# Masked attention after a group normalization: group statistics by transposes and GpSimd sums, and a split of the score products in two visits

## The chip, the cores and the metric

One core of one Trainium2 chip runs the whole kernel. Its engines are TensorE (PE in the profile, with PEld for its weight loads), VectorE (DVE), ScalarE (ACT), GpSimd (POOL) and SyncE (SP). Each takes its instructions in program order from its own queue, and they wait for each other by semaphores. The metric is the device time of one execution in microseconds (us), as the median of several runs.

## What is computed

The input is x, 32 images of 256 channels and 32 x 32 pixels in float32. A group normalization over 32 groups of 8 channels comes first, then attention of 8 heads of 32 channels with a strictly lower mask, and the input is added to the result:

```python
def _gn(v, G=32, eps=1e-5):                      # 8 channels x 1024 pixels a group
    g = v.reshape(B_, G, C_ // G, H_, W_)
    m = jnp.mean(g, axis=(2, 3, 4), keepdims=True)
    s = jnp.var(g, axis=(2, 3, 4), keepdims=True)
    return ((g - m) / jnp.sqrt(s + eps)).reshape(v.shape)

q, k, v = ...                                     # 1x1 convolutions with bias
scores = jnp.einsum('bhqd,bhkd->bhqk', q, k) / jnp.sqrt(dk)
attn = softmax(where(mask == 0, -10000, scores)); attn = where(mask == 0, 0, attn)
out = jnp.einsum('bhqk,bhkd->bhqd', attn, v)
return x + out
```

A channel is a partition, and the 256 channels are two tiles of 128 (g = 0, 1). So a group is 8 neighbouring partitions, and its statistics need a sum over partitions. Mean and variance of each channel come first. The group's mean is the mean of the channels' means, and its variance is the mean of the channels' variances plus the mean of the squared deviations of their means.

## The kernel before

An image is worked off in 12 visits: 6 for each half of the heads (4 heads, g = 0, 1). The main loop (L750 to L769) runs over all 384 visits and one more. At step i it emits the scores of visit i, then what is planned `at` i (a projection of the next image, above all), then the values of visit i - 1, then what is planned `between`, then the additions of keys of visit i - 1, and at last what is planned `after` i. The order is written out by hand for all five engines (`tc.manual_schedule`), so what stands earlier in this program stands earlier in each engine's queue.

**A visit.** `scores` (L348) computes transposed scores of 4 heads into three PSUM tiles: heads 0, 1 long, heads 2, 3 long, and the short remainders of all four. A product of one head takes 32 rows of PE and 64 of its columns, in two halves, so several run side by side. The order is: short products of heads 2, 3; long ones of heads 0, 1; long ones of heads 2, 3; a wait until the first short ones are done (`bank_free`, L379); short products of heads 0, 1. Where a visit has two long entries and is in `PAIRS` (visits 0 and 6), one long entry of heads 0, 1 stands between the two short ones of heads 2, 3 (L364). ACT takes three exponentials of each visit (L397 twice, L393). In visits 0, 1, 3, 4 of each half, `mask` (L329) has POOL make a triangle of the diagonal blocks by two selects (L339), one for each 128 columns. `values` (L412) multiplies the exponentials with v on PE; the diagonal products come after the others, each behind its select. `add_keys` (L434) sums exponentials on DVE (L440), and POOL's DMAs fold these sums over partitions (`fold`, L449). `finish` (L539) normalizes with the inverse sums and adds x, on DVE.

**Preparation of the next image.** `prepare` (L637) plans it over the visits of the image before, by `PREPARE` (L652): channel statistics of g = 0 and 1 on DVE after visits 0 and 1 (`norm_channels`, L179); the product with `avg` that gives the groups' means between values and additions of step 3 (`norm_mean`, L187: PE, then ACT writes minus the mean); the deviations on DVE in the same place (`norm_deviation`, L198); a second product and ACT's copy after step 4 (`norm_variance`, L210); the power -1/2 and the shift on POOL, also after step 4 (`norm_rstd`, L221); and from step 5 ACT's normalization of x (`norm_apply`, L231), whose results the projections take from step 7. The product with `avg` is four PE instructions of 128 rows by 32 columns; each is done in two passes, so the profile counts eight.

The selects of a visit are emitted with its scores. What POOL is given `after` step 2 or 3 therefore stands in its queue ahead of the selects of visit 3 or 4, and behind those of the visits up to then. At step 3, `after` also holds the second fold of an earlier image's last sum, which is planned first.

The tile `turned` (L465, one buffer) holds transposed sums in steps 6 and 7.

Of the kernel before, what the change touches and what calls it, by code (L numbers as in the profile page):

```python
# [32 lines left out]
def tile_norm_attention_residual(  # L33
# [65 lines left out]
    def unshifted():  # L99
# [79 lines left out]
        def norm_channels(b, g):  # L179
            if g == 0:  # L180
                live["mv", b] = small.tile([P, NG, 2], F32, tag="mv", name=f"mv_{b}")
            st = small.tile([P, NH, 6], F32, tag="st", name=f"st_{b}_{g}")
            for c in range(NH):
                nc.vector.bn_stats(st[:, c, :], live["x", b][:, g, c * HALF : (c + 1) * HALF])
            nc.vector.bn_aggr(live["mv", b][:, g, :], st)

        def norm_mean(b):  # L187
            mv = live["mv", b]
            pm = misc(f"pm_{b}")
            product(pm[:, :NG], avg, mv[:, :, 0])  # L190
            if b == 0:
                live["dev", b] = small.tile([P, NG], F32, tag="dev", name=f"dev_{b}")
                nc.vector.tensor_sub(live["dev", b], mv[:, :, 0], pm[:, :NG])
            mean = small.tile([P, NG], F32, tag="mean", name=f"mean_{b}")
            nc.scalar.activation(mean, pm[:, :NG], AF.Identity, scale=-1.0)
            live["minus_mean", b] = mean

        def norm_deviation(b):  # L198
            mv, minus_mean = live["mv", b], live["minus_mean", b]

            if b == 0:
                dev = live["dev", b]
            else:
                dev = small.tile([P, NG], F32, tag="dev", name=f"dev_{b}")
                nc.vector.tensor_add(dev, mv[:, :, 0], minus_mean)
            nc.vector.tensor_mul(dev, dev, dev)
            nc.vector.tensor_add(dev, dev, mv[:, :, 1])
            live["dev", b] = dev

        def norm_variance(b):  # L210
# [4 lines left out]
            if b == 0:  # L215

                nc.vector.tensor_scalar_add(rstd, pv[:, :NG], 1e-5)
                return
            nc.scalar.activation(rstd, pv[:, :NG], AF.Identity, bias=eps)

        def norm_rstd(b):  # L221
            rstd = live["rstd", b]
            if b == 0:

                nc.gpsimd.tensor_tensor(rstd, rstd, power, ALU.pow)
                return
            nc.gpsimd.tensor_tensor(rstd, rstd, power, ALU.pow)
# [100 lines left out]

        def mask(b, g, raw, j):  # L329
# [18 lines left out]
        def scores(b, v):  # L348
# [15 lines left out]
            if i in PAIRS and len(longs) > 1:  # L364
# [227 lines left out]
        PAIRS = {0: 0, 1: 1, 3: 3, 4: 2}  # L592

# [38 lines left out]
        at, between, after = {}, {}, {}  # L632
# [4 lines left out]
        def prepare(b, whens):  # L637
            for n, f in zip(whens, [
                lambda: norm_channels(b, 0), lambda: norm_channels(b, 1), lambda: norm_mean(b),
                lambda: norm_deviation(b), lambda: norm_variance(b), lambda: norm_rstd(b),  # L640
            ] + [lambda hf=hf, g=g: norm_apply(b, hf, g) for hf in range(NH) for g in range(NG)]):
                if n is None:
                    f()
                elif isinstance(n, tuple):
                    when(n[0], f, between)
                else:
                    when(n, f, after)
# [4 lines left out]
        PREPARE = (-12, -11, -9, -9, -8, -8, -7, -6, -5, -3)  # L652
# [4 lines left out]
        every = range(4)  # L657
        ALIGN = 24, 64

        with tc.manual_schedule(engines={ENG.PE, ENG.Activation, ENG.DVE, ENG.Pool, ENG.SP}):  # L660
# [43 lines left out]
            if B > 1:  # L704
                prepare(1, (None, None, 0, 1, 2, 2, 3, 4, 5, 7))
            for b in range(B):
# [4 lines left out]
                if b >= 2:  # L711
# [6 lines left out]
                    prepare(b, [(first + n,) if k in (2, 3) else first + n for k, n in enumerate(PREPARE)])  # L718
# [31 lines left out]
            for i in range(B * N + 1):  # L750
# [8 lines left out]
                if i:  # L759
                    values(b, v)  # L760
                    for f in between.pop(i, ()):
                        f()
# [7 lines left out]
            assert not at and not between and not after  # L770
# [174 lines left out]
```

## Time and profile before

| | |
|---|---|
| Time, median of 3 runs | 1794.0 us (1793.49 to 1794.12) |
| The profiled execution | 1793.44 us, its span 1791.7 us |
| Mean granted clock of PE | 0.999 |
| One image | 55.09 us |

How to read the profile: its times are from one execution. A row of the timeline gives start, duration, engine, line, operation, the tiles written and read, how many instructions are merged, and in brackets the idle time before with what ended it. The durations of DVE and POOL include time in which an instruction had begun and could not go on. Ends of matmuls are modelled. The groups that belong to the statistics, from the list of groups by form:

```profile
L169 PE MATMUL pm<-mv,avg 128*32 128x2 f32 x256 | 7.0, 170 | 0.0
L169 PE MATMUL pv<-dev,avg 128*32 128x2 f32 x256 | 7.1, 170 | 0.5 <-ACT k L258 0.4
L195 ACT ACTIVATE mean<-pm 128x2 f32<-128x2 f32 x32 | 5.5, 172 | 29.6 <-PE pm L169 25.9 <-DVE dev L193 3.6
L219 ACT ACTIVATE rstd<-pv,eps 128x2 f32<-128x2 f32 x31 | 8.1, 263 | 13.4 <-PE pv L169 13.4
L504 DVE STREAM_TRANSPOSE inv_turned<-inv 128x64 f32<-128x64 f32 x31 | 7.6, 245 | 1.1
```

The last is a transpose that is there already; it is shown for its duration.

### The profile page before, as it was taken

The page shows a single profiled execution, that of the slowest core. Times are in us where ns is not written, and L with a number is a line of the kernel's source. Part 1 is how long each engine was busy: PE and PEld are TensorE (multiplying, and loading weights), DVE is VectorE, ACT ScalarE, POOL GpSimd, SP SyncE. Part 2 cuts the span into 40 slices and gives each one's busy share as a digit, 9 for nine tenths or more (in the row PEclk, how much of TensorE's full clock was granted, in tenths as well). Part 3 has the DMA queues.
Part 4 walks back from the last instruction along what each step waited for, and adds up shares of the span by engine and source line. Part 5 has one row for each costly group of instructions (what it writes and reads, how often), then busy time and mean ns, then how long its engine had stood idle before and what let it go on. Part 6 is the DMA issues. An engine that isn't in the chain of part 4 may idle for free.

```text
span 1791.7 us, 81825 instructions
## 1 busy us (share of the span) xinstructions
PE 1784.4 (100%) x37036; PEld 948.2 (53%) x37036; DVE 1673.4 (93%) x1826; ACT 1456.4 (81%) x1990; POOL 881.3 (49%) x903
## 2 busy tenths in 40 slices
PE   9999999999999999999999999999999999999998
PEld 5555555555555555555555555555555555555554
DVE  4689999999999999999999999999999999999998
ACT  6888878888788888788887888878888878888785
POOL 2345544554545555445554455454555544555452
PEclk9999999999999999999999999999999999999999
DMA  2566766767667766766676676767776667666664
GB/s 70 105 115 137 134 134 129 147 135 143 127 126 149 140 138 134 135 139 138 139 135 131 129 150 132 145 125 128 149 141 135 136 134 138 139 139 137 132 107 106
DMA packets 86818, 236.77 MB, mean 132 GB/s; under 512 B 21312, under 2 KB 22336, under 8 KB 70592
## 3 DMA queue, kind: packets, MB, share of 16 engines
q0 software_dynamic: 15872, 97.53, 40.1%
q1 hardware_dynamic: 70448, 133.89, 25.5%
q8 instruction: 290, 4.75, 1.1%
q14 instruction: 64, 0.52, 0.1%
q10 hardware_dynamic: 144, 0.07, 0.0%
HBM read 66.85 MB, written 34.57 MB: 57 GB/s over the span
## 4 chain that ended last, share of the span: by engine, by line
PE 99%; ACT 0%; DVE 0%; issue 0%; POOL 0%; POOLq 0%
PE sT L311 31%; PE acc L422 28%; PE pp L169 26%; PE ppv L169 13%; PE pd L474 1%; PE busy L155 0%; ACT e L397 0%; PE pv L169 0%; PE pm L169 0%; PE wt L148 0%; DVE rb_last L547 0%; ACT eh L393 0%; DVE rb_last L534 0%; DVE turned L531 0%; DVE acc L544 0%
## 5 line engine op out<-in xcount | busy, mean ns | idle before, releaser
L339 POOL TENSOR_SCALAR_AFFINE_SELECT diagonal<-eh 128x512 f32<-128x512 f32 x512 | 632.5, 1256 | 841.5 <-ACT eh L393 840.9
L397 ACT ACTIVATE e<-sT 128x1024 f32<-128x1024 f32 x768 | 744.4, 1022 | 250.3 <-PE sT L311 225.9
L440 DVE TENSOR_TENSOR e<-e,e 128x1024 f32<-128x1024 f32 x314 | 574.2, 1829 | 24.5 <-ACT v L275 3.2
L311 PE MATMUL sT<-q,k 32*64 32x128 f32 (+2 forms) x18432 | 578.4, 372 | 0.1
L311 PEld LDWEIGHTS sT<-q,k 32*64 32x64 f32 x18432 | 394.8, 131 | 188.4 <-PE sT L311 69.6
L169 PE MATMUL pp<-xn,wT 128*32 128x512 f32 x4096 | 492.2, 598 | 0.0
L422 PE MATMUL acc<-e,v 128*32 128x512 f32 (+3 forms) x4608 | 401.0, 450 | 0.0
L393 ACT ACTIVATE eh<-sT 128x768 f32<-128x768 f32 (+1 forms) x384 | 341.7, 890 | 0.0
L422 PEld LDWEIGHTS acc<-e,v 128*32 128x32 f32 x4608 | 149.2, 110 | 261.5 <-issue 238.9
L169 PE MATMUL ppv<-wT,xn 128*32 128x256 f32 x4096 | 247.5, 382 | 0.0
L440 DVE TENSOR_TENSOR diagonal<-diagonal,e 128x1536 f32<-128x1536 f32 x126 | 195.0, 1548 | 16.8 <-PE acc L422 9.2
L169 PEld LDWEIGHTS pp<-xn,wT 128*32 128x32 f32 x4096 | 107.0, 109 | 195.7 <-issue 163.7
L440 DVE TENSOR_TENSOR e<-e,eh 128x1024 f32<-128x1024 f32 x126 | 164.2, 1303 | 6.5
L422 PEld LDWEIGHTS acc<-diagonal,v 128*32 128x32 f32 x4096 | 121.1, 110 | 87.6 <-issue 76.0
L440 DVE TENSOR_TENSOR e<-e,diagonal 128x2048 f32<-128x2048 f32 x63 | 144.2, 2289 | 19.8 <-POOL diagonal L339 19.8
L169 PEld LDWEIGHTS ppv<-wT,xn 128*32 128x32 f32 x4096 | 120.1, 109 | 79.7 <-issue 7.0
L422 PE MATMUL acc<-diagonal,v 128*32 128x128 f32 x4096 | 158.7, 273 | 0.0
L244 ACT ACTIVATE xn<-x,shift,rstd 128x256 f32<-128x256 f32 x248 | 136.8, 608 | 0.6 <-POOL shift L229 0.6
L544 DVE TENSOR_TENSOR num<-num,rb 128x512 f32<-128x512 f32 x124 | 123.3, 994 | 0.2 <-DMA rb<-inverses 0.2
L453 POOL DMA_DIRECT2D e<-e x124 | 103.3, 833 | 38.2 <-issue 38.2
L547 DVE SCALAR_TENSOR_TENSOR rb<-num,v_bias_col,x 128x256 f32<-128x256 f32 x248 | 117.5, 515 | 4.4
L453 POOL DMA_DIRECT2D diagonal<-diagonal x124 | 104.1, 839 | 4.8 <-issue 4.8
(84 smaller groups left out, 984.4 us busy)
## 6 DMA issues: line engine op xcount, KB each, us to landing
x<-in_x_dram SPq DMA_DIRECT2D x124, 256.0 KB, 3.7
diagonal<-diagonal POOLq DMA_DIRECT2D x62, 512.0 KB, 5.4
e<-e POOLq DMA_DIRECT2D x62, 512.0 KB, 5.9
rb<-inverses SPq DMA_DIRECT2D x124, 256.0 KB, 3.9
out_dram<-rb SPq DMA_DIRECT2D x124, 256.0 KB, 4.9
diagonal<-diagonal POOLq DMA_DIRECT2D x62, 256.0 KB, 4.6
folded<-diagonal SPq DMA_DIRECT2D x62, 256.0 KB, 5.1
e<-e POOLq DMA_DIRECT2D x62, 256.0 KB, 5.0
```

The costliest lines, as they stand in the source:

```text
L169: nc.tensor.matmul(out[part], lhsT=lhsT[:, part], rhs=rhs, start=start, stop=stop, skip_group_check=True)
L244: nc.scalar.activation(to, of, AF.Identity, bias=live["shift", b][:, g : g + 1], scale=rstd)
L311: return nc.tensor.matmul(bank[c : c + KEYS, cols], lhsT=live["k", b, g][rows, kb * P + c : kb * P + c + KEYS], rhs=live["q", b, g][rows, ...
L339: nc.gpsimd.affine_select(out=square[:, :, place + s * P : place + (s + 1) * P], in_=raw[:, :, (1 - s) * KEYS : (3 - s) * KEYS], pattern=[ ...
L393: exp = nc.scalar.activation(eh.rearrange("p (n bank) q -> p bank n q", n=2)[:, :, :, :narrow], short[:, :, :, :narrow], AF.Exp)
L397: nc.scalar.activation(e[:, 2 * a : 2 * a + 2, :wide], pairs[a][:, :, :wide], AF.Exp)
L422: nc.tensor.matmul(acc[HD * j : HD * (j + 1), of], lhsT=live["v", b][:, kb, h * HD : (h + 1) * HD], rhs=e[:, j, :], start=first, stop=last ...
L440: nc.vector.tensor_add(to, to, tile_of(b, g, at))
L453: nc.gpsimd.dma_start(out=total[:rows], in_=total[rows : 2 * rows], accum_op=ALU.add)
L474: nc.tensor.matmul(pd[HD * j : HD * (j + 1), of], lhsT=pick, rhs=e[:, j, :], start=start, stop=stop, skip_group_check=True,)
L544: nc.vector.tensor_mul(num, num, rb)
L547: nc.vector.scalar_tensor_tensor(blocks(rb, s), blocks(num, s, (start + s) % 2 == 1), v_bias_col[:, g : g + 1], blocks(xt[:, g, cols], s), ...
```

## The change

For the images after the first (their statistics are prepared 31 times), the group sums leave PE and ACT. The channels' means and variances are written into the first 4 columns of a tile `stats` (the buffer of `turned`), whose columns up to 32 POOL has set to 0. A DVE transpose of 32 columns turns each block of 32 channels, so that the 8 channels of a group lie beside each other. `group_means` (POOL, after step 2) sums them by three additions, spreads minus the mean, subtracts and squares: six operations. `group_deviations` (POOL, after step 3) does three additions and one spreading operation. `group_variance` (DVE, also after step 3) transposes 64 columns back and subtracts. `norm_rstd` stays as it was. The first image is prepared as before.

In visits 3 and 4 of each image but the last (`SPLIT`), the long product of heads 0, 1 of 512 columns becomes one of 128 and one of 384, and the first stands between the two short ones of heads 2, 3, as in visit 0. In values of visits 2 and 8 PE gets one more wait each (`EVEN`), for a value of `bank_free` for which the scores ahead of them have waited.

```diff
         def norm_channels(b, g):
             if g == 0:
-                live["mv", b] = small.tile([P, NG, 2], F32, tag="mv", name=f"mv_{b}")
+                if b == 0:
+                    live["mv", b] = small.tile([P, NG, 2], F32, tag="mv", bufs=1, name=f"mv_{b}")
+                else:
+                    stats = live["stats", b] = small.tile([P, HALF], F32, tag="turned", bufs=1, name=f"stats_{b}")
+                    nc.gpsimd.memset(stats[:, 2 * NG : HD], 0.0)
+                    live["mv", b] = stats[:, : 2 * NG].rearrange("p (g s) -> p g s", s=2)
...
+            if b and g == NG - 1:
+                stats = live["stats", b]
+                nc.vector.transpose(stats[:, HD : 2 * HD], stats[:, :HD])
+
+        def sum_eight(b, out, of, work):
+            of = of.rearrange("p (n c) -> p n c", c=CPG)
+            half = work[:, : HD // 2].rearrange("p (n c) -> p n c", c=CPG // 2)
+            pairs = work[:, HD // 2 : 3 * HD // 4].rearrange("p (n c) -> p n c", c=CPG // 4)
+            nc.gpsimd.tensor_tensor(half, of[:, :, : CPG // 2], of[:, :, CPG // 2 :], ALU.add)
+            nc.gpsimd.tensor_tensor(pairs, half[:, :, : CPG // 4], half[:, :, CPG // 4 :], ALU.add)
+            nc.gpsimd.tensor_tensor(out, pairs[:, :, 0], pairs[:, :, 1], ALU.add)
...
+        def group_means(b):
+            of, means, dev, work = (live["stats", b][:, n * HD : (n + 1) * HD] for n in (1, 2, 6, 7))
+            sums = work[:, 3 * HD // 4 : 3 * HD // 4 + HD // CPG]
+            sum_eight(b, sums, of, work)
+            nc.gpsimd.tensor_scalar(
+                means.rearrange("p (n c) -> p n c", c=CPG), spread_of(sums), -1.0 / CPG, None, ALU.mult
+            )
+            nc.gpsimd.tensor_tensor(dev, of, means, ALU.add)
+            nc.gpsimd.tensor_tensor(dev, dev, dev, ALU.mult)
+
+        def group_deviations(b):
+            squares, dev, work = (live["stats", b][:, n * HD : (n + 1) * HD] for n in (3, 6, 7))
+            sums = work[:, 3 * HD // 4 : 3 * HD // 4 + HD // CPG]
+            sum_eight(b, sums, dev, work)
+            nc.gpsimd.tensor_scalar(
+                squares.rearrange("p (n c) -> p n c", c=CPG), spread_of(sums), 1.0 / CPG, 1e-5, ALU.mult, ALU.add
+            )
+
+        def group_variance(b):
+            stats = live["stats", b]
+            nc.vector.transpose(stats[:, 4 * HD : 6 * HD], stats[:, 2 * HD : 4 * HD])
+            means, squares = (
+                stats[:, n * HD : n * HD + 2 * NG].rearrange("p (g s) -> p g s", s=2) for n in (4, 5)
+            )
+            live["minus_mean", b] = means[:, :, 0]
+            live["rstd", b] = small.tile([P, NG], F32, tag="rstd", name=f"rstd_{b}")
+            nc.vector.tensor_sub(live["rstd", b], squares[:, :, 0], means[:, :, 1])
...
+        def part_of(b, g, bank, entry, of):
+            at, _, halves = entry
+            for j in (0, 1):
+                for ((c, kb, first, _, cols),) in halves:
+                    score(b, g, bank[:, j, :], j, (
+                        c, kb, first + of.start, of.stop - of.start, slice(cols.start + of.start, cols.start + of.stop)
+                    ))
...
             begin = [lambda n=n: long_of((0, 1), n) for n in range(len(longs) - 1, -1, -1)]
-            if i in PAIRS and len(longs) > 1:
+            if b < B - 1 and v in SPLIT:
+                begin = [lambda n=n: part_of(b, g, pairs[0], longs[0], n) for n in (slice(0, P), slice(P, HALF))]
+            if i in PAIRS and len(begin) > 1:
                 first = short_of((2, 3), begin.pop(0), slice(None, None, -1))
...
+        SPLIT = 3, 4
...
-                lambda: norm_channels(b, 0), lambda: norm_channels(b, 1), lambda: norm_mean(b),
-                lambda: norm_deviation(b), lambda: norm_variance(b), lambda: norm_rstd(b),
+                lambda: norm_channels(b, 0), lambda: norm_channels(b, 1), lambda: group_means(b),
+                lambda: group_deviations(b), lambda: group_variance(b), lambda: norm_rstd(b),
...
-        PREPARE = (-12, -11, -9, -9, -8, -8, -7, -6, -5, -3)
+        PREPARE = (-12, -11, -10, -9, -9, -8, -7, -6, -5, -3)
...
+        EVEN = 2, 8
...
-                prepare(1, (None, None, 0, 1, 2, 2, 3, 4, 5, 7))
+                prepare(1, (None, None, 0, 1, 1, 2, 3, 4, 5, 7))
...
-                    prepare(b, [(first + n,) if k in (2, 3) else first + n for k, n in enumerate(PREPARE)])
+                    prepare(b, [first + n for n in PREPARE])
...
                 if i:
+                    for _ in range(EVEN.count((i - 1) % N) if i < B * N - N else 0):
+                        nc.tensor.wait_ge(bank_free, live["free"])
                     values(b, v)
-                    for f in between.pop(i, ()):
-                        f()
```

`spread_of(sums)` is a view that repeats each sum for the 8 channels of its group.

More of the change, by code (lines that the diff above doesn't have):

```diff
@@ L185, in norm_channels, with spread_of @@
             nc.vector.bn_aggr(live["mv", b][:, g, :], st)
+            if b and g == NG - 1:
[8 more added lines that the diff above has]
+            nc.gpsimd.tensor_tensor(out, pairs[:, :, 0], pairs[:, :, 1], ALU.add)
+        def spread_of(sums):
+            return sums.unsqueeze(2).broadcast_to([P, HD // CPG, CPG])
+        def group_means(b):
[23 more added lines that the diff above has]
+            nc.vector.tensor_sub(live["rstd", b], squares[:, :, 0], means[:, :, 1])
         def norm_mean(b):
@@ L190, in norm_mean @@
             product(pm[:, :NG], avg, mv[:, :, 0])
[L191 to L194, printed above, removed]
+            live["dev", b] = small.tile([P, NG], F32, tag="dev", bufs=1, name=f"dev_{b}")
+            nc.vector.tensor_sub(live["dev", b], mv[:, :, 0], pm[:, :NG])
+            mean = small.tile([P, NG], F32, tag="mean", bufs=1, name=f"mean_{b}")
             nc.scalar.activation(mean, pm[:, :NG], AF.Identity, scale=-1.0)
@@ L198, in norm_deviation @@
         def norm_deviation(b):
[L199 to L205, printed above, removed]
+            mv, dev = live["mv", b], live["dev", b]
             nc.vector.tensor_mul(dev, dev, dev)
             nc.vector.tensor_add(dev, dev, mv[:, :, 1])
-            live["dev", b] = dev
         def norm_variance(b):
@@ L214, in norm_variance @@
             live["rstd", b] = rstd
[L215 to L219, printed above, removed]
+            nc.vector.tensor_scalar_add(rstd, pv[:, :NG], 1e-5)
         def norm_rstd(b):
             rstd = live["rstd", b]
+            nc.gpsimd.tensor_tensor(rstd, rstd, power, ALU.pow)
             if b == 0:
-                nc.gpsimd.tensor_tensor(rstd, rstd, power, ALU.pow)
                 return
-            nc.gpsimd.tensor_tensor(rstd, rstd, power, ALU.pow)
             live["shift", b] = small.tile([P, NG], F32, tag="shift", name=f"shift_{b}")
@@ L631, in unshifted @@
         }
-        at, between, after = {}, {}, {}
+        at, after = {}, {}
         def when(i, f, where=at):
@@ L643, in prepare @@
                     f()
-                elif isinstance(n, tuple):
-                    when(n[0], f, between)
                 else:
@@ L769, in unshifted @@
                     f()
-            assert not at and not between and not after
+            assert not at and not after
             inside = end_last(B - 1)
```

## The prediction

> **What bounds the kernel now.** I read the page first, then the busy time of one image, then the timelines of PE, GpSimd (POOL), VectorE (DVE) and ScalarE (ACT) over that image. From the page: the span, PE's busy time, and the engines' shares of the chain that ended last.
>
> ```profile
> span 1791.7 us, 81825 instructions
> ...
> PE 1784.4 (100%) x37036; PEld 948.2 (53%) x37036; DVE 1673.4 (93%) x1826; ACT 1456.4 (81%) x1990; POOL 881.3 (49%) x903
> ...
> PE 99%; ACT 0%; DVE 0%; issue 0%; POOL 0%; POOLq 0%
> ```
>
> PE is the chain, and it never stops: each image takes the same 55.09 us. So a microsecond leaves the time only where PE has less to do, and one is added only where PE is made to wait. The second engine is the one to watch. One image, busy us of PE, PEld, DVE, ACT, POOL:
>
> ```profile
> 958.20:1013.30 55.10, 55.10 (x1158) 29.27 (x1152) 52.90 (x58) 45.44 (x63) 27.99 (x28) 1.00 0.70 137
> ```
>
> DVE has only 2.2 us free in 55, mostly in gaps of 0.1 us and less, and one real wait (0.53 us). Now the timelines around the change, of visits 2 to 4 of one image: DVE, then POOL, then PE.
>
> ```profile
> 969.73 0.21 DVE L185 BATCH_NORM_AGGREGATE mv<-st 128x2 f32<-128x12 f32 x1
> 969.93 3.09 DVE L440 TENSOR_TENSOR diagonal<-diagonal,e 128x1536 f32<-128x1536 f32 x2
> 972.94 1.12 DVE L544 TENSOR_TENSOR num<-num,rb 128x512 f32<-128x512 f32 x1
> 974.10 1.13 DVE L547 SCALAR_TENSOR_TENSOR rb<-num,v_bias_col,x 128x256 f32<-128x256 f32 x2
> ...
> 975.77 1.23 DVE L440 TENSOR_TENSOR e<-e,e 128x1024 f32<-128x1024 f32 x1
> 976.91 1.22 DVE L440 TENSOR_TENSOR e<-e,eh 128x1024 f32<-128x1024 f32 x1
> 978.16 2.60 DVE L440 TENSOR_TENSOR e<-e,e 128x2048 f32<-128x2048 f32 x1
> ```
>
> ```profile
> 972.55 2.00 POOL L339 TENSOR_SCALAR_AFFINE_SELECT diagonal<-eh 128x512 f32<-128x512 f32 x2 [6.30 <-ACT eh L393]
> 974.51 0.82 POOL L453 DMA_DIRECT2D e<-e  x1
> 977.58 3.68 POOL L339 TENSOR_SCALAR_AFFINE_SELECT diagonal<-eh 128x512 f32<-128x512 f32 x2 [2.25 <-ACT eh L393]
> 981.23 1.15 POOL L227 TENSOR_TENSOR rstd<-rstd,power 128x2 f32<-128x2 f32 x1
> 982.46 0.31 POOL L229 TENSOR_TENSOR shift<-mean,rstd 128x2 f32<-128x2 f32 x1
> ```
>
> ```profile
> 973.50 0.22 PE L169 MATMUL pm<-mv,avg 128*32 128x2 f32 x8
> ...
> 977.67 0.62 PE L422 MATMUL acc<-diagonal,v 128*32 128x128 f32 x16
> ...
> 982.33 0.62 PE L422 MATMUL acc<-diagonal,v 128*32 128x128 f32 x16
> ```
>
> See the slack of the masks: that of visit 3 ends on POOL at 974.55, and PE wants its halves at 977.67 and 977.89. That of visit 4 ends at 981.26, and PE wants its second half at 982.55. And see that from 969.93 on DVE runs additions and multiplications back to back.
>
> **How small POOL operations fare beside DVE.** The same instruction pair in an earlier image:
>
> ```profile
> 98.87 0.72 POOL L227 TENSOR_TENSOR rstd<-rstd,power 128x2 f32<-128x2 f32 x1
> 99.67 1.62 POOL L229 TENSOR_TENSOR shift<-mean,rstd 128x2 f32<-128x2 f32 x1
> ```
>
> Two numbers per partition cost 0.31 us in most images and 1.62 here, where a DVE addition of 2048 ran from 98.94 to 101.23. The shift ended 0.06 us after it: it stood still until about 0.13 us before the addition's recorded end, and took 0.185 itself.
>
> **What the Trainium skill says.** "SBUF — State Buffer", section Who interferes with whom: a DVE instruction with two SBUF inputs contends with a GpSimd instruction that reads SBUF, and the second to issue waits for all of the first. The trace agrees: 1.62 against 0.31 above, and a select of 0.62 alone takes up to 2.7. "GPSIMD Engine Reference", section 2.1 Instruction dispatch: a GpSimd instruction that reads what another core wrote in the one before it needs a wait on that one's semaphore. Here the dependent shift starts 0.08 after the power ends. The same page's section 3.1 prices a two-input operation at about 2.6 cycles an element; with the 0.185 above I estimate 0.20 to 0.25 us for 4 to 32 elements. "VectorE: DVE Perf Modes", section The three transpose paths: the DVE transpose works in 32x32 blocks, as the change uses it; the trace has 0.245 us for 64 columns, so about 0.21 for 32.
>
> **The change part by part.**
>
> *PE, statistics.* Eight instructions of pm and eight of pv leave each of 31 images. With pm, values of visit 2 last until the scores 0.036 us longer than values of visit 8, which have no pm (1.871 against 1.835 between the same starts); pv costs 0.035. Gain 0.071.
>
> *PE, split.* In visits 3 and 4 heads 0, 1 begin 0.054 us after heads 2, 3 now (eight products are dealt out first, 0.0067 each); with the narrow short first and 128 columns next, 0.027. Two more passes cost 0.0025 each (128 columns 0.109, 512 columns 0.429). Gain 0.022 a visit, 0.044 an image. The other bound is visit 0, already split, with 1.42 us for its scores against 1.40 here: a loss of 0.015 a visit. I take the gain, because visit 0's delay comes at its end, where its second long product meets the short ones; that part isn't copied.
>
> *PE, waits.* The two added waits ask for what the scores before them already waited for, and the two stand-alone waits of pm and pv leave. Cover: PE's queue handles such a wait 1.7 us before its product starts. Without it 2 x 0.05 x 31 = 3 us.
>
> *ACT* loses mean (0.17) and rstd (0.26); it waits for PE there, so nothing. *POOL's memset* (0.13) falls into a wait of 1.57 in visit 0: nothing. Of DVE, three operations on dev (0.5) go, two transposes and a subtraction (0.6) come.
>
> PE's part: -0.071 - 0.044 = -0.115 an image, -3.6 us in all.
>
> *POOL's chain, means.* Six dependent operations are queued ahead of the mask of visit 3. The first waits for the transpose, done at 970.19, and then the first addition (1.76) has started. After each DVE release one POOL operation runs, and while its successor waits 0.08 for it, DVE has started its next: it restarts 0.05 to 0.23 after a release, POOL needs about 0.28. So: op 1 at 971.81 (first addition), op 2 at 973.14 (second, 1.23), op 3 at 973.74 (the multiplication, 0.68 alone), op 4 at 974.26 and op 5 at 974.68 (the two of L547, 0.48 each), op 6 at 976.00 (the addition now at 975.77, earlier by the dev operations gone), ending 976.25. The select then waits for the next addition: its halves end at 977.76 and 978.35 instead of 974.55. PE, due at 977.59 and 977.81, waits 0.23 and then 0.37 (a signal takes 0.06): **0.60**.
>
> *Deviations.* Behind the mask stands the fold's DMA (0.82, to 979.13), then four operations: 0.22 + 0.20 + 0.20 + 0.34 and three gaps of 0.08, to 980.33. DVE, done at 977.27, stands still, because the transpose in its queue waits for them, and behind that every addition. That makes POOL quick, but the addition of 2.29 starts at 980.79, just before the second half of the visit-4 mask asks; this ends at 983.57. PE wants it at 983.03 (982.55 - 0.12 + 0.60): **0.60** more.
>
> *Shift.* Power and shift come behind that, at about 985.1 instead of 982.77. ACT has two xn operations (1.10) that wait for it, ahead of the exponentials of the next visit:
>
> ```profile
> 984.07 1.94 ACT L397 ACTIVATE e<-sT 128x1024 f32<-128x1024 f32 x2 [0.17 <-PE sT L311]
> 985.89 0.82 ACT L393 ACTIVATE eh<-sT 128x768 f32<-128x768 f32 x1
> ```
>
> These would be ready at 985.15 (984.07 + 1.08) and start at 986.13, 0.98 late. PE's next scores need the third of them and have 0.65 to spare: **0.33**. What ACT and DVE still owe after that is between 0 and 0.5; I take 0.10.
>
> Sum: 0.60 + 0.60 + 0.33 + 0.10 - 0.115 = 1.52 us an image, x 31 = 47. The profiled execution took 1793.4 us (span 1791.7, and 1.7 around it), 0.6 under the median of 1794.0. 1793.4 + 47 = **1840**; own range 1824 to 1856 (1.0 to 2.0 an image).
>
> **The rivals.**
> 1. *Two close starts fall the other way.* Op 2 misses the second addition by 0.07 us, op 6 and the select the next by about as little. If both get in first, the visit-3 mask is in time; DVE still stands for about 1 us, against 0.53 of real wait, and the second mask is close. +0.2 to +0.6 an image: about 1806.
> 2. *All is hidden, not slower.* POOL is busy 49%, and the visit-3 mask has about 3 us of slack. If a small operation got in between two DVE operations each time, the six would take 1.8 us and fit before 972.55. Then PE's gain stands: 1793.4 - 3.6 = 1789.8. It decides where an operation with its gap takes under about 0.15 us; against it, 0.185 + 0.08 from the trace.
> 3. *DVE becomes the bound.* It stands 3.2 us an image, and had 2.2 free. If none of this is won back from shorter contention, 2.5 an image: 1871.
>
> **How the numbers follow.** Forecast 0.60, rival 1 0.15, rival 2 0.20, rival 3 0.05. About 0.2% (3.6 us) is what a measurement can tell from no change, and rival 2 lies on that line: 0.11 faster, 0.09 same. Slower: 0.80. The range 1790 to 1856 holds most of the forecast, rival 1 and half of rival 2.
>
> **What would show it.** Right: POOL's chain of six takes over 5 us, each operation ending just after a DVE one; visit 3's selects start after 975; PE waits for diagonal in two places of every image; DVE idles before the 64-column transpose; the image period is 56 to 57 us. Wrong: six operations within 2 us, a period of 54.97, or PE waiting somewhere else.

## The result, and the profile after

| | before | after |
|---|---|---|
| Time, median of 6 runs | 1793.49 us (1793.34 to 1794.12) | 1834.03 us (1833.16 to 1834.86) |
| The profiled execution, its span | 1793.44, 1791.7 us | 1833.16, 1831.5 us |
| One image (typical) | 55.09 us | 56.45 us |

The ratio is 1.0225, with a 95% interval of 1.0212 to 1.0238. The change makes the kernel slower by 2.2%. First the page of the changed kernel: span, busy time, and the engines' shares of the chain that ended last, with its first lines.

```profile
span 1831.5 us, 82103 instructions
...
PE 1798.7 (98%) x37036; PEld 925.9 (51%) x37036; DVE 1627.7 (89%) x1826; ACT 1433.9 (78%) x1928; POOL 1122.4 (61%) x1244
...
POOL 40%; DVE 24%; issue 15%; PE 14%; ACT 5%; POOLq 1%; DMA 1%; DVEq 0%; SPq 0%; ACTq 0%
POOL diagonal L386 23%; DVE e L489 14%; PE sT L349 4%; PE acc L471 4%; DVE st L189 4%; PE pp L169 4%; POOL e L502 4%; POOL stats L200 3%; DVE rb L596 3%; ACT e L446 3%; POOL stats L201 2%; DVE num L593 2%; PE ppv L169 2%; POOL stats L217 2%
```

PE held 99% of the chain before, and now has 14%: POOL and DVE set the end between them, in turns. PE is 98% busy all the same. The instruction counts of PE are the same in both kernels. Now POOL's timeline over visits 2 to 4 of one image (start, duration, engine, line, operation, tiles; in brackets the idle time before and what ended it).

```profile
1047.23 1.77 POOL L200 TENSOR_TENSOR stats<-stats 128x16 f32<-128x16 f32 x1 [4.70 <-DVE stats L193]
1049.08 1.24 POOL L201 TENSOR_TENSOR stats<-stats 128x8 f32<-128x8 f32 x1
1050.39 0.53 POOL L202 TENSOR_TENSOR stats<-stats 128x4 f32<-128x4 f32 x1
1051.01 0.52 POOL L213 TENSOR_SCALAR stats<-stats 128x32 f32<-128x32 f32 x1
1051.62 0.27 POOL L216 TENSOR_TENSOR stats<-stats 128x32 f32<-128x32 f32 x1
1051.96 1.11 POOL L217 TENSOR_TENSOR stats<-stats 128x32 f32<-128x32 f32 x1
1053.02 2.20 POOL L386 TENSOR_SCALAR_AFFINE_SELECT diagonal<-eh 128x512 f32<-128x512 f32 x2
1055.18 0.84 POOL L502 DMA_DIRECT2D e<-e  x1
1055.81 0.47 POOL L200 TENSOR_TENSOR stats<-stats 128x16 f32<-128x16 f32 x1
1056.36 0.20 POOL L201 TENSOR_TENSOR stats<-stats 128x8 f32<-128x8 f32 x1
1056.64 0.20 POOL L202 TENSOR_TENSOR stats<-stats 128x4 f32<-128x4 f32 x1
1056.94 0.21 POOL L223 TENSOR_SCALAR stats<-stats 128x32 f32<-128x32 f32 x1
1057.21 3.35 POOL L386 TENSOR_SCALAR_AFFINE_SELECT diagonal<-eh 128x512 f32<-128x512 f32 x2
```

The timeline of DVE over the same stretch:

```profile
1046.93 0.21 DVE L193 STREAM_TRANSPOSE stats<-stats 128x32 f32<-128x32 f32 x1
1047.16 3.09 DVE L489 TENSOR_TENSOR diagonal<-diagonal,e 128x1536 f32<-128x1536 f32 x2
1050.17 0.69 DVE L593 TENSOR_TENSOR num<-num,rb 128x512 f32<-128x512 f32 x1
1050.89 0.88 DVE L596 SCALAR_TENSOR_TENSOR rb<-num,v_bias_col,x 128x256 f32<-128x256 f32 x2
1051.69 0.15 DVE L601 COPY rb<-x 128x1 f32<-128x1 f32 x1
1051.75 1.22 DVE L489 TENSOR_TENSOR e<-e,e 128x1024 f32<-128x1024 f32 x1
1052.89 1.26 DVE L489 TENSOR_TENSOR e<-e,eh 128x1024 f32<-128x1024 f32 x1
1057.18 0.24 DVE L231 STREAM_TRANSPOSE stats<-stats 128x64 f32<-128x64 f32 x1 [3.03 <-POOL stats L223]
1057.45 0.41 DVE L237 TENSOR_TENSOR rstd<-stats 128x2 f32<-128x2 f32 x1
1057.79 2.28 DVE L489 TENSOR_TENSOR e<-e,e 128x2048 f32<-128x2048 f32 x1
```

Read the two together. The addition of 16 numbers per partition (L200) takes 1.77 us while DVE does its first addition of the 3.09, and 0.47 when DVE stands. Those of 8 and of 4 take 1.24 and 0.53 beside DVE and 0.20 each when it stands. The first six operations last 5.84 us (1047.23 to 1053.07), where they would take under 2 (an estimate from the 0.20 to 0.47 of the second four and the gaps of 0.08 between them). Each of the six ends 0.06 to 0.16 us after an instruction of DVE: the third, for one, at 1050.92, after the multiplication L593 at 1050.86. The two selects of visit 3 start right behind them. DVE then waits 3.03 us for the second four. That makes these quick, but the second select of visit 4 (begun at 1057.80) meets DVE's next addition (begun at 1057.79), so the two take 3.35 us. PE pays for the late selects; its timeline at the values of visits 3 and 4 of the image before:

```profile
998.25 0.43 PE L471 MATMUL acc<-diagonal,v 128*32 128x128 f32 x8 [0.18 <-POOL diagonal L386]
998.83 0.42 PE L471 MATMUL acc<-diagonal,v 128*32 128x128 f32 x8 [0.16 <-POOL diagonal L386]
...
1003.27 0.40 PE L471 MATMUL acc<-diagonal,v 128*32 128x128 f32 x8
...
1004.16 0.42 PE L471 MATMUL acc<-diagonal,v 128*32 128x128 f32 x8 [0.49 <-POOL diagonal L386]
```

The gaps in brackets start at modelled ends of products, so they are shorter than the waits. PE's time for each part, between starts of products in a typical image (us), shows the waits whole:

| | before | after | difference |
|---|---|---|---|
| values of visit 2 (with pm before) | 1.871 | 1.835 | -0.036 |
| scores of visit 3 | 1.403 | 1.388 | -0.015 |
| values of visit 3 (with pv before) | 1.443 | 2.169 | +0.726 |
| scores of visit 4 | 1.410 | 1.388 | -0.022 |
| values of visit 4 | 1.408 | 2.110 | +0.702 |

These add to +1.355, the whole of 56.45 - 55.09. Without pv the values of visit 3 would take 1.408, so PE waits 0.76 there and 0.70 in visit 4. Image 0 has none of it (-0.71), nor image 1 (-0.11), in which DVE has no earlier image to finish. From the start of image 0 to that of image 31 it is 1750.1 - 1710.6 = 39.5 us.

### The profile page after: what moved, and what is told of

Same layout as the page of the kernel before. It is cut to its first block, busy times and chain, and to the rows that moved or that the text cites. A ratio compares the mean times of both kernels' runs of the same rounds, so it can differ in the third digit from the quotient of the medians.

```text
span 1831.5 us, 82103 instructions
## 1 busy us (share of the span) xinstructions
PE 1798.7 (98%) x37036; PEld 925.9 (51%) x37036; DVE 1627.7 (89%) x1826; ACT 1433.9 (78%) x1928; POOL 1122.4 (61%) x1244
## 4 chain that ended last, share of the span: by engine, by line
POOL 40%; DVE 24%; issue 15%; PE 14%; ACT 5%; POOLq 1%; DMA 1%; DVEq 0%; SPq 0%; ACTq 0%
POOL diagonal L386 23%; DVE e L489 14%; PE sT L349 4%; PE acc L471 4%; DVE st L189 4%; PE pp L169 4%; POOL e L502 4%; POOL stats L200 3%; DVE rb L596 3%; ACT e L446 3%; POOL stats L201 2%; DVE num L593 2%; PE ppv L169 2%; POOL stats L217 2%; POOL rstd L263 2%
## 5 line engine op out<-in xcount | busy, mean ns | idle before, releaser
L386 POOL TENSOR_SCALAR_AFFINE_SELECT diagonal<-eh 128x512 f32<-128x512 f32 x512 | 683.7, 1357 | 488.2 <-ACT eh L442 486.0
L349 PE MATMUL sT<-q,k 32*64 32x64 f32 (+1 forms) x18928 | 577.7, 367 | 0.5 <-issue 0.3
L489 DVE TENSOR_TENSOR e<-e,e 128x1024 f32<-128x1024 f32 x314 | 551.3, 1756 | 22.2 <-ACT v L313 3.2
L489 DVE TENSOR_TENSOR diagonal<-diagonal,e 128x1536 f32<-128x1536 f32 x126 | 201.3, 1597 | 15.5 <-PE acc L471 7.7
L471 PE MATMUL acc<-diagonal,v 128*32 128x128 f32 x4096 | 172.0, 275 | 23.9 <-POOL diagonal L386 23.6
L471 PEld LDWEIGHTS acc<-diagonal,v 128*32 128x32 f32 x4096 | 115.3, 110 | 135.3 <-POOL diagonal L386 73.1
L200 POOL TENSOR_TENSOR stats<-stats 128x16 f32<-128x16 f32 x62 | 64.6, 1042 | 135.9 <-DVE stats L193 135.9
L502 POOL DMA_DIRECT2D e<-e x124 | 103.7, 837 | 39.5 <-issue 37.5
L596 DVE SCALAR_TENSOR_TENSOR rb<-num,v_bias_col,x 128x256 f32<-128x256 f32 x248 | 110.3, 486 | 4.4
```

Source lines behind the costliest of these rows:

```text
L200: nc.gpsimd.tensor_tensor(half, of[:, :, : CPG // 2], of[:, :, CPG // 2 :], ALU.add)
L349: return nc.tensor.matmul(bank[c : c + KEYS, cols], lhsT=live["k", b, g][rows, kb * P + c : kb * P + c + KEYS], rhs=live["q", b, g][rows, ...
L386: nc.gpsimd.affine_select(out=square[:, :, place + s * P : place + (s + 1) * P], in_=raw[:, :, (1 - s) * KEYS : (3 - s) * KEYS], pattern=[ ...
L471: nc.tensor.matmul(acc[HD * j : HD * (j + 1), of], lhsT=live["v", b][:, kb, h * HD : (h + 1) * HD], rhs=e[:, j, :], start=first, stop=last ...
L489: nc.vector.tensor_add(to, to, tile_of(b, g, at))
L502: nc.gpsimd.dma_start(out=total[:rows], in_=total[rows : 2 * rows], accum_op=ALU.add)
```

## The experiments

The theory after that: POOL's first six operations are held up by DVE's instructions with two SBUF inputs, one per DVE instruction; so the selects queued behind them are late, and PE waits. The rivals: that POOL's queue or its number of instructions does it; that DVE's standing is the loss, as DVE has so little free; and that the split costs instead of gaining. Unless something else is said, edits are to the changed kernel.

**1. The split alone.** The kernel before with `part_of` and `SPLIT`, and nothing else of the change.

```diff
+            if b < B - 1 and v in SPLIT:
+                begin = [lambda n=n: part_of(b, g, pairs[0], longs[0], n) for n in (slice(0, P), slice(P, HALF))]
+        SPLIT = 3, 4
```

> The kernel before with the split of visits 3 and 4 alone (statistics as before). My theory: the split shortens the scores of these two visits by about 0.02 us each and causes no wait, so 31 x 0.04 = 1.3 us less than before, 1792.2 us. Rival (the split is what slows: more products, another order at the banks): at least 20 us more than before.

Measured: 1799.16 us (1797.54 to 1801.41), ratio 1.0025 (1.0015 to 1.0036): slower by 0.25%, and a miss, as 1792.2 was expected. Most images take 55.05 us, 0.04 less than before, as worked out for the split. But nine of 31 take up to 1.8 us more, together 8.4 us. PE in the timeline of such an image:

```profile
784.37 1.14 PE L311 MATMUL sT<-q,k 32*64 32x128 f32 x24
...
786.55 1.09 PE L311 MATMUL sT<-q,k 32*64 32x512 f32 x24 [1.04 <-issue]
```

PE stops for a microsecond in the middle of one visit's products, and "issue" says that it waited for nothing that the profile shows. The stops come in visit 1 of images 3, 10, 11, 18 and 25, and at the scores of visit 10 in images 13, 14, 27 and 28: every 7 or 8 images and every 14. The page of the same run, in its part on DMA queues (packets, MB, share):

```profile
q8 instruction: 294, 4.82, 1.1%
```

Here 4.82 MB in 294 packets are 16.4 KB each. PE has about 75,100 instructions in this kernel, so a packet holds 256 of them at 64 bytes. An image has 2338 instructions of PE here (2 x 1168 and two waits), 34 more than 9 x 256. So the place where a packet begins walks through the images, and is back after 256 / 34 = 7.5 of them. The changed kernel and the one before both have 2306.

That the stop belongs to the packet can be read from the traces. Number the records of PE (weight loads, products, waits) in the order of the program, from 0. Over the traces of all runs, PE has 19 gaps of more than 0.12 us inside the loop that end with "issue". In all 19 the product behind the gap has a number that leaves 192 when it is divided by 256; that of the gap above is 32704 = 127 x 256 + 192. So these stops come at one place in every 256 instructions, and at most of these places there is none.

**2. The statistics alone.**

```diff
-        SPLIT = 3, 4
+        SPLIT = ()
```

> The changed kernel without the split (the statistics on VectorE and GpSimd stay). My theory: the same two waits of PE for the selects in each image, and 1.3 us of gain lost: 1835.3 us. Rival (the split slows): 1795 us or less.

Measured: 1839.28 us (1835.16 to 1839.66), ratio 1.0244 (1.0228 to 1.0259), 4 us over what was expected. The typical image takes 56.45 us, so the loss is all in the statistics. The count is 2274 here, 30 under 9 x 256, and the stops come in images 6, 14, 15, 24 (visits 0 and 1) and 10, 19, 27 (visit 10): 256 / 30 = 8.5 apart. In the profiled execution the stretch from the last image on was 2.8 us longer too: PE's branch at L967 took 4.37 us there, and 0.38 in the changed kernel. In that execution the stops in the loop took 2.7 us; stops and end together cover the 4 us.

**3. POOL only writes.** The ten operations become memsets of the same sizes; the first six wait for the same transpose, and DVE transposes as before. The group sums are left out.

```diff
-            sum_eight(b, sums, of, work)
...
+            for n in (16, 8, 4, HD):
+                nc.gpsimd.memset(of[:, :n], 0.0)
+            for _ in range(2):
+                nc.gpsimd.memset(means, 0.0)
```

> The ten sums on GpSimd of each image become ten memsets of the same sizes with the same waits (the group statistics are left out: mean 0, variance 1). They stand in the same places of the queue, but read nothing from SBUF. My theory (each small operation stands still behind a VectorE operation with two SBUF inputs): the six take about 1.2 us instead of 5.8, both selects are in time, and the time is 1790 us, before's less the gain on PE. Rival (ten more dependent instructions in GpSimd's queue cost this by themselves, reads or not): the time stays within 8 us of 1834.

Measured: 1789.84 us (1789.61 to 1792.04), ratio 0.9977 (0.9967 to 0.9986). Each image takes 54.98 us, which is 55.09 - 0.11, PE's gain by itself. POOL's timeline in one image:

```profile
915.53 0.61 POOL L198 MEMSET stats<- 128x16 f32 x4 [4.06 <-DVE stats L193]
916.08 0.31 POOL L200 MEMSET stats<- 128x32 f32 x2
917.75 2.71 POOL L366 TENSOR_SCALAR_AFFINE_SELECT diagonal<-eh 128x512 f32<-128x512 f32 x2 [1.36 <-ACT eh L422]
```

Six memsets take 0.86 us, the later ones beside DVE's addition, which begins at 915.84. The selects again wait for their data, and not for the queue. As many instructions in the same queue cost nothing, so it is their reading that is held up. The memsets don't depend on each other, as the sums do; but that isn't what costs, since the second four sums of the changed kernel, just as dependent, took 0.20 each while DVE stood. This is what the Trainium skill's page "SBUF — State Buffer" has in Who interferes with whom: the contention is with a GpSimd instruction that reads, and not with one that only writes.

**4. The sums on VectorE.** Two reductions, two `tensor_scalar`, an addition and a square on DVE in the places of POOL's ten operations.

```diff
-            sum_eight(b, sums, of, work)
-            nc.gpsimd.tensor_scalar(
...
+            nc.vector.tensor_reduce(sums, of.rearrange("p (n c) -> p n c", c=CPG), AX.X, ALU.add)
+            nc.vector.tensor_scalar(
...
```

> The sums move from GpSimd to VectorE: two reductions over 8, two spreading operations, one addition and one square in place of ten GpSimd operations; the places in the program stay. My theory: no select is late, and VectorE pays about 0.7 us an image more than before, against 0.5 of real wait and 2.2 in all that it has free: between 1790 and 1810 us, 1797 likeliest. Rival (VectorE's load and its two transposes in the way are what slows): 1825 us or more.

Measured: 1833.18 us (1831.77 to 1833.64), ratio 1.0216 (1.0200 to 1.0231). A miss: no faster than POOL's. The masks of visits 3 and 4 are in time, but PE now waits at the values of visit 6 (0.5 us), the scores of visit 11 (0.7) and the values of visit 10 (0.2). One line of ACT's timeline tells for whom:

```profile
967.92 1.94 ACT L435 ACTIVATE e<-sT 128x1024 f32<-128x1024 f32 x2 [2.70 <-DVE diagonal L478]
```

The exponentials wait for a buffer that DVE has yet to add up. At the values of visits 6 and 10 PE waits for selects of POOL again, other ones than before: DVE's additions come later, and the selects of visit 6 are held up beside them for 4.15 us, against 3.42 in run 3.

```profile
950.90 4.15 POOL L375 TENSOR_SCALAR_AFFINE_SELECT diagonal<-eh 128x512 f32<-128x512 f32 x2 [2.81 <-ACT eh L431]
...
955.14 0.65 PE L460 MATMUL acc<-diagonal,v 128*32 128x128 f32 x16 [0.30 <-POOL diagonal L382]
```

Against run 3, DVE has 1.3 us more work per image (0.18, 0.18, 0.19, 0.19, 0.17 and 0.40), and the image takes 56.43 us, 1.45 more.

**5. VectorE does not stand.** The transpose back reads columns that DVE wrote itself. POOL does its ten operations for nobody, so this kernel leaves the group sums out of its result.

```diff
-            nc.vector.transpose(stats[:, 4 * HD : 6 * HD], stats[:, 2 * HD : 4 * HD])
+            nc.vector.transpose(stats[:, 4 * HD : 6 * HD], stats[:, : 2 * HD])
...
```

> The changed kernel, but the transpose back on VectorE reads columns that VectorE itself wrote (the channels' own statistics), so that it no longer waits for GpSimd; GpSimd does all ten operations as before, for nobody. Group statistics are left out. Theory (the ten GpSimd operations hold up the two masks, VectorE's standing is harmless in itself): GpSimd's first six operations are held up as in the changed kernel, so the 0.76 us of visit 3 stays; the four deviations lose the 3 us in which VectorE stood still and are held up too, so visit 4 loses 0.70 us or more; period 56.4 to 57.5 us, total 1830 to 1865 us. Rival (the 3.0 us in which VectorE stands each image are what sets the time, the engine being nearly full): period back to about 55 us, total 1790 to 1800 us.

Measured: 1883.72 us (1877.12 to 1889.34), ratio 1.0499 (1.0475 to 1.0524): slower by a further 2.7%. So the standing isn't the loss. The period (one image) is 57.7 us in most images, 59.2 in others. POOL, DVE and PE in the timeline of one image:

```profile
672.92 4.32 POOL L386 TENSOR_SCALAR_AFFINE_SELECT diagonal<-eh 128x512 f32<-128x512 f32 x2
...
674.47 2.28 DVE L489 TENSOR_TENSOR e<-e,e 128x2048 f32<-128x2048 f32 x1
...
676.67 1.11 DVE L593 TENSOR_TENSOR num<-num,rb 128x512 f32<-128x512 f32 x1
...
677.29 0.43 PE L471 MATMUL acc<-diagonal,v 128*32 128x128 f32 x8 [2.28 <-POOL diagonal L386]
```

The selects of visit 3, already late, now meet DVE's next addition and take 4.32 us instead of 2.20; PE waits 2.7 us there. I had put that loss at visit 4, where there is none, and its size was outside what I had written. While DVE stands, it keeps off these selects.

**6. VectorE loaded by itself.** Run 3 (so without the group sums) with four memsets of 128 x 320 on DVE, ahead of the transpose back.

```diff
+            for _ in range(4):
+                nc.vector.memset(stats[:, 6 * HD :], 0.0)
```

> The run with memsets for GpSimd's sums (1789.8 us, period 54.98 us), with four memsets of 128 x 320 more on VectorE per image, ahead of the transpose back; they only write and wait for nothing. I take 0.3 to 0.4 us for each, 1.2 to 1.6 us per image. Group statistics are left out. Theory from the run with the sums on VectorE (VectorE has no more than some 0.2 us per image to spare, so work added to it is paid in full): period 56.0 to 56.5 us, total 1822 to 1838 us. Rival (that run was slow because of its chain of dependent small operations or their reads, not for VectorE's time): total 1790 to 1795 us.

Measured: 1826.11 us (1825.63 to 1826.69), ratio 1.0181 (1.0165 to 1.0196). The four take 4 x 0.325 = 1.3 us (1.6 with the gaps between them), and the image 56.15 instead of 54.98, 1.17 more. So only 0.1 to 0.4 us of DVE was free. PE loses it in the same three places as in run 4: 0.29 us at the values of visit 6, 0.70 at the scores of visit 11, 0.17 at the values of visit 10. So DVE's time is enough to explain run 4, without anything that its sums read. How much of it is DVE's time itself, and how much the selects that then meet later additions, was not told apart.

**7 to 10. A version that reads less.** If four operations of POOL stood there instead of ten, the select behind them would be in time. That can be had by summing the mean square with the mean, instead of the deviations after it: the group's variance is the mean of (variance + mean squared) less the square of the group's mean. DVE forms minus (variance + mean squared) of each channel ahead of the transpose, POOL sums both columns in one go, and DVE takes the square off at the end.

```diff
-            nc.gpsimd.tensor_tensor(dev, of, means, ALU.add)
-            nc.gpsimd.tensor_tensor(dev, dev, dev, ALU.mult)
-        def group_deviations(b):
...
+            nc.vector.tensor_mul(squares, mv[:, :, 0], mv[:, :, 0])
+            nc.vector.scalar_tensor_tensor(
+                out=mv[:, :, 1], in0=squares, scalar=-1.0, in1=mv[:, :, 1], op0=ALU.mult, op1=ALU.subtract
+            )
...
+            nc.vector.tensor_mul(squares, both[:, :, 0], both[:, :, 0])
+            nc.vector.scalar_tensor_tensor(
+                out=live["rstd", b], in0=both[:, :, 1], scalar=1e-5, in1=squares, op0=ALU.add, op1=ALU.subtract
+            )
```

The first form of it still had one more POOL operation, ahead of the power:

```diff
+                nc.gpsimd.tensor_scalar(rstd, rstd, -1.0, 1e-5, ALU.mult, ALU.add)
```

> The statistics in one pass: VectorE forms variance + mean squared of each channel (two operations of 128 x 1) before the transpose, GpSimd sums both columns at once in four operations instead of ten, and VectorE takes the mean's square off after the transpose back (two operations of 128 x 1 instead of one of 128 x 2). Theory (the masks of visits 3 and 4 are late because of the GpSimd operations queued before them): the four operations end at the place where the changed kernel's fourth ended, 1.5 us before its mask of visit 3 could start, which covers the 0.76 us; the mask of visit 4 has nothing before it; VectorE does not stand. Period 55.0 to 55.4 us, total 1788 to 1803 us, 1793 likeliest, as VectorE gets some 0.4 us of small operations more than in the run with memsets. Rival (any sums on GpSimd in that place, or any addition to VectorE, cost the same again): 1815 to 1835 us.

Measured: 1794.96 us (1793.04 to 1796.85), ratio 1.0005 (0.9996 to 1.0013). All images but three take 55.1 us or less; image 1 takes 58.83, since that operation was held up for 2.28 us, the power for 2.85 and the shift for 1.25, and ACT waited 3.51 for the shift. Without it, and DVE adding the 1e-5 (the diff above):

> The statistics in one pass again, without what made the run before it lose 3.9 us in image 1: there GpSimd had an operation more ahead of the power (2.28 us, held up), so that the shift came 3.5 us late once. Here the signs are arranged so that VectorE gives variance + 1e-5 itself (two operations of 128 x 2 ahead of the transpose, two after the transpose back), and GpSimd has the power and the shift alone. Theory: all images at 54.98 us, total that of the run with memsets, 1790 us (1788.5 to 1792), 0.1 to 0.3% below the kernel before. Rival (the real sums still hold up a mask or a shift in some images, or VectorE's small operations tell): 1793 to 1800 us.

Measured: 1793.71 us (1792.10 to 1796.12), ratio 0.9999 (0.9990 to 1.0007). In the profile the images are where they were expected (31 take 1706.9 us, against 1710.6 before), but the time isn't: from the start of the last image on it took 67.6 us instead of 65.2. The gap is at the program's end, at one POOL instruction that has nothing to wait for. Two runs on that; first six waits per image more on POOL, meant to give it as many instructions as in the changed kernel. In the trace they are three instructions per image: 1450 records of POOL, against 1357 without them and 1543 in the changed kernel.

```diff
+                    for _ in range(6):
+                        nc.gpsimd.wait_ge(live["arrived"], 1)
```

> The one-pass statistics of the run before (1793.7 us, though 31 images took 1706.94 us there against 1710.57 in the kernel before), with six waits per image on GpSimd, on a semaphore long reached, at the start of the statistics, so that GpSimd gets as many instructions as in the changed kernel. Theory (the loop is right and 2.45 us were lost at the very end, where GpSimd's last wait came 3.8 us after the branch ahead of it with nothing to wait for, so for its instructions): the end is short again, 1789.5 to 1792 us, 0.1 to 0.25% below the kernel before. Rival (the end or the images stall in another place, as the one-pass kernel's 93 more instructions on VectorE stay): 1792.5 to 1796 us, no different from before.

Measured: 1792.81 us (1792.01 to 1796.96), ratio 0.9996 (0.9988 to 1.0004). The end still took 66.8 us; the gap (1.7 us) came two instructions later. Then fewer waits on POOL at the start of the program; in the trace that is 8 records less:

```diff
-        ALIGN = 24, 64
+        ALIGN = 24, 48
```

> The kernel of the run before (1792.8 us) with 16 waits fewer on GpSimd at the start of the program (48 instead of 64), which changes nothing else. There the gap of 1.7 us on GpSimd at the end of the program had moved by two instructions against the run before it, as the number of GpSimd instructions had changed. Theory (a block of its instructions is fetched there, and the place goes by the count): the boundary falls 16 instructions later, behind the program's last, the end is as short as in the run with memsets (65.1 us from the start of the last image), total 1790.5 to 1792 us, 0.1 to 0.2% below the kernel before. Rival (the gap belongs to the branch ahead of it and not to the count): the end stays 1.6 us or more longer, 1792 to 1794 us.

Measured: **1790.70 us** (1789.94 to 1792.20), ratio 0.9982 (0.9975 to 0.9989), and an end of 65.15 us. This version beats both kernels: it is 0.2% below the one before, and 2.4% below the changed one (0.9982 / 1.0225). It is the fourth try, and its end was tuned by hand; in its loop 31 images take 1708.4 us. POOL's timeline in it:

```profile
915.12 1.76 POOL L203 TENSOR_TENSOR stats<-stats 128x16 f32<-128x16 f32 x1 [5.08 <-DVE stats L196]
916.96 1.24 POOL L204 TENSOR_TENSOR stats<-stats 128x8 f32<-128x8 f32 x1
918.28 0.53 POOL L205 TENSOR_TENSOR stats<-stats 128x4 f32<-128x4 f32 x1
918.90 0.52 POOL L214 TENSOR_SCALAR stats<-stats 128x32 f32<-128x32 f32 x1
919.39 2.34 POOL L384 TENSOR_SCALAR_AFFINE_SELECT diagonal<-eh 128x512 f32<-128x512 f32 x2
```

The four operations are held up as in the changed kernel, to within 0.01 us (1.77, 1.24, 0.53, 0.52). The contention has not gone; there is only less behind which the selects stand, and that is enough: they start 1.5 us earlier than behind six, where PE had waited 0.76. The page's chain is PE's again:

```profile
PE 99%; DMA 0%; DVE 0%; ACT 0%; issue 0%; SPq 0%; ACTq 0%
```

**11 and 12. The instruction counts by themselves.** Two runs on what run 1 had shown, both made from run 3. One adds waits to PE, which change nothing else. The text asks for 32 more per image, but in the trace there are 13 more (15 instead of 2; several that stand together for the same value leave fewer). So an image has 2319 instructions of PE, 15 more than 9 x 256, and not the 2338 that was expected:

```diff
-        EVEN = 2, 8
+        EVEN = (2, 8) + tuple(n % 11 for n in range(32))
```

> The run with memsets for GpSimd's sums (1789.8 us, 2306 TensorE instructions per image), with 32 more waits per image on TensorE, all on a semaphore long reached, up to three in front of the values of a visit. Group statistics are left out. Theory (the run with the split alone was slow because its 2338 instructions per image are 34 more than 9 x 256: its stalls of 0.6 to 1.8 us without any releaser came in visits 1 and 10 of images 3, 10, 11, 18, 25 and 13, 14, 27, 28, that is about every 256/34 = 7.5 and every 15 images): stalls come back at that spacing, total 1794 to 1800 us. Rival (the stalls belong to the eight products added there): none here, 1790 us.

Measured: 1794.30 us (1791.52 to 1799.14), against 1789.84 for run 3. Most images still take 54.98 us, so 13 waits cost nothing in themselves. But PE stops again, in images 7, 14 and 23 (visits 0 and 1) and in 10, 13 and 29 (visit 10). So stops come back, as the theory had it, without the products of the split. The spacing expected (7.5 images) went with the wrong count; for 15 it is 256 / 15 = 17, and 7 to 23 and 13 to 29 are 16 each. Those of images 13 and 14 stand at 192 in the count, and that of image 10 within four of it. The other takes the two waits of the change away (2304, just 9 x 256):

```diff
-        EVEN = 2, 8
+        EVEN = ()
```

> The run with memsets for GpSimd's sums (1789.8 us, 2306 TensorE instructions per image) without the two added waits per image on TensorE, so 2304 = 9 x 256. Group statistics are left out. Theory (what counts is how far the number is from a multiple of 256): the place of a block's start no longer moves from image to image, so stalls come in no image or in all: 1789 to 1791 us, or above 1810 us. Rival (the two waits do something in themselves, such as pacing the values of visits 2 and 8): a loss of some us, spread unevenly over the images, 1792 to 1800 us.

Measured: 1790.09 us (1789.49 to 1790.96), no different from run 3. So the two waits are worth nothing here, as the prediction had it. What matters is that the split brings 32 instructions and pm and pv take 32 away.

## Why the prediction was right

It was right in its direction, its main mechanism and its size: 1840 against 1834, with the time inside its own range, and every sign that it had named for being right is there. That it came so near is in part luck, as one step was wrong. By its steps:

- *PE, statistics and split*: 0.071 + 0.044 = 0.115 an image, measured 0.071 and 0.037 to 0.041. Run 3 has it alone: 0.11. What it left out is that the split could be had at this price only together with the removal of pm and pv; alone it lost 5 us (run 1).
- *POOL's chain, means*: six operations to 6.06 us after the transpose; measured 5.93 (1047.14 to 1053.07), each released by the DVE instruction that the prediction named. The selects end 8.08 us after the transpose (8.16 predicted). PE's wait was **mis-sized: 0.76, not 0.60**. As the selects were not later than predicted, PE asked for them earlier, in relation to the transpose, than the prediction had it: the transpose ends 1.78 us after the scores of visit 3 begin, where the prediction's 970.19 is 1.57 after.
- *Deviations*: quick because DVE stands, for 3.03 us (3.2 predicted). The second mask ends 13.42 us after the transpose (13.38 predicted). PE's wait was **0.70, not 0.60**; the 0.21 by which PE asks earlier, the 0.04 by which the mask is later, and the 0.16 more that PE has already waited in visit 3 make 0.69.
- *Shift*: this step failed, at the wait. ACT did wait for the shift, 1.85 us, and the exponentials of visit 6 came 0.95 us late (1006.66 instead of 1005.7). But PE did not wait. ACT and PE in the timeline of that image:

```profile
1005.66 1.09 ACT L282 ACTIVATE xn<-x,shift,rstd 128x256 f32<-128x256 f32 x2 [1.85 <-POOL shift L267]
...
1006.66 1.91 ACT L446 ACTIVATE e<-sT 128x1024 f32<-128x1024 f32 x2
...
1008.46 0.81 ACT L442 ACTIVATE eh<-sT 128x768 f32<-128x768 f32 x1
...
1009.09 1.47 PE L349 MATMUL sT<-q,k 32*64 32x128 f32 x48
```

  The prediction said that PE's next scores need the third exponential, and had 0.65 us to spare. It took the wrong products. The three PSUM tiles of a visit share three buffers, and in the program built from this kernel they rotate: the first products of visit 7 (the short ones of heads 2, 3) write where the first exponential of visit 6 has read, and only the long ones of heads 2, 3 write where the third has. By their records those long products begin 0.53 us after the first, at 1009.62, and the third exponential ends at 1009.27; in the kernel before it was 987.99 and 986.71. So the spare time was about 1.2 us, more than the delay of 0.95. The 0.33, and the 0.10 owed after it, are 0.
- *The sum*: 0.76 + 0.70 - 0.11 = 1.35 an image against 1.52, and 29 images pay it, not 31. Two errors of +0.26 and -0.43 partly cancelled.

Of the rivals, the close starts (1) fell as the forecast had them: op 2 was held by the second addition, op 6 by the one at 1051.75, and the select by the one at 1052.89. "All is hidden" (2) is what run 3 gives, with operations that don't read. "DVE the bound" (3) was no bound here, but its premise was right, and tighter than it had it: 0.1 to 0.4 us of DVE's time is to be had, and not 2.2 (run 6). (Its 2.5 us an image is not worked out; 3.2 of standing less 2.2 free would be 1.0.) In the changed kernel ACT already waits for it:

```profile
ACT e L446 <- DVE diagonal L489: 28.2, 29, 1.5
```

That is about 1 us in each image. It does not reach PE: the two waits for selects are the whole of what an image takes longer.

## What to carry to other kernels

Here a chain of small dependent GpSimd operations beside a full VectorE cost about one VectorE instruction with two SBUF inputs for each operation, so price such a chain by what VectorE does at that time and not by its own size; then look at what stands behind it in GpSimd's queue. Cut the number of operations that read, or let them only write; moving them to the full engine gained nothing here. Where TensorE is the bound, keep its number of instructions per pass of the loop, or count what an edit does to it.

## What was not expected of the hardware

- TensorE's instructions come in packets of 256 (16.4 KB), and PE can stop once in such a packet, for 0.2 to 1.8 us: all 19 gaps of PE without a releaser stand at the same number, 192, modulo 256. With 2306 or 2304 instructions per image that cost 0 to 2.4 us in the profiled executions; with 2338 it cost 8.4 in run 1, and some 4.5 of the median with 2319, by waits that do nothing (run 11). Why only some packets bring a stop, and why those in visits 0, 1 and 10, was not tried.
- A gap of this kind at the end of the program was worth 2 us, and moved with GpSimd's number of instructions (67.6, 66.8, 65.15 us for the last stretch). In run 2 it was TensorE's (67.95 us), with GpSimd's number as in the changed kernel. What the size of a packet is on GpSimd stays open, so that this gap is for instructions is not shown.
- 13 more waits on TensorE, of 51 ns each by their records, cost an image nothing (54.98 us with and without).
- The two selects of 128 x 512 of a visit took GpSimd 2.20 us where VectorE did one more addition and then stood, and 4.32 us where it went on, in the same place of the loop.
